# A graph network's prologue: inverse roots by Newton's steps, the first pair of tiles projected ahead of the edge work, edge counts and their gathers moved forward

## The chip, the cores and the metric

The kernel runs on one NeuronCore of a Trainium2 chip, in one launch. The metric is device time in microseconds (us). Engines: PE is TensorE's matmul, PEld its weight load, DVE VectorE, ACT ScalarE, POOL GpSimd, SP SyncE, which here only issues DMAs. ACT and POOL issue DMAs too (ACTq, POOLq and SPq in the profile). Each engine works through its own queue in order; semaphores join the queues.

## The reference

Two layers on x, 3125 nodes of 256 features each: a graph diffusion and a mixture of experts, each on a normalized input and added to what it reads. 103125 directed edges (src, dst), sorted by dst.

```
def _layernorm(x, eps=1e-05):
    m = mean(x, -1);  v = var(x, -1)
    return (x - m) / sqrt(v + eps)

def _spmm(h, src, dst, inv_deg):
    return segment_sum(h[src], dst, 3125) * inv_deg[:, None]

def gnn(h):
    h = silu(h @ W_in.T + b_in)
    out = term = h
    for i in range(1, 7):                       # K_STEPS = 6
        term = _spmm(term, src, dst, inv_deg) / i
        out = out + term
    return out @ W_out.T + b_out

x = x + gnn(_layernorm(x))
x = x + moe(_layernorm(x))                      # 8 experts, the 2 best of each row, 256 -> 512 -> 256
```

The change touches only the beginning: the first layer norm, the projections and the reading of the edges. All else runs the same instructions.

## The kernel before

Nodes stand in 25 tiles of 128 rows (the last has 53). The output projection commutes with the diffusion, so it is applied first: each tile is normalized, multiplied by W_in, put through SiLU, multiplied by W_out, and kept in `t0` as two halves of a number each (a rounded value and what it leaves out, 2 x 256 columns). Then step 1 of the diffusion builds, tile by tile, a dense block of the adjacency matrix out of the edges by products of 0/1 matrices on PE, writes it to memory, and multiplies it with `t0`. Steps 2 to 6 read the blocks back and multiply. In the last step rows are routed to experts, whose matmuls end the kernel.

The prologue, which is all that the change touches, has two strands.

*The projection of tiles.* Tiles of x are loaded into `acc` by SP in groups of 2, 4, 6, 6, 6 and the last one (L321 to L327). DVE takes mean and variance of each (`bn_stats` and `bn_aggr`, L556 and L557, into `mv`). In three batches, tiles 0 to 1, 2 to 5 and 6 to 24, ACT takes the square root of the variance (L558), and DVE its reciprocal `rstd` and the offset `shift` (L559, L560). `normed(t)` (L563 to L573) lets ACT normalize a pair of tiles into `xn` and PE transpose it into `pt`, one pair ahead of its use. The loop over 13 pairs (L576 to L596) copies `pt` to `xt` (ACT, L579), multiplies by `w_in_sb` into `ph` (PE, L586; two halves c, each followed by a SiLU on ACT, L588, into `ht`), multiplies by `w_out_sb` into `pm` (PE, L593), and splits the result into `t0` (DVE, L595 a copy, L596 a subtraction). `ph`, `pm`, `xn`, `xt` and `ht` have one buffer each, `pt` two.

*The edges.* ACT's queue loads `di` (dst) and `si` (src), 128 x 818 numbers each. DVE and ACT cut them into three small parts (L417 to L422), PE transposes these (L433), ACT (parts 0 and 2) and DVE (part 1) copy them side by side into `pairs` (L436, L437), and two DMAs on ACT's queue write the list `edges` of triples to memory (L439, L441). Beside it DVE counts where each group of 16 nodes begins: `first_i` holds the first dst of each chunk of 128 edges; the counts `below` (L447) give a chunk number, POOL gathers that chunk's dst numbers into `row_i` (L455), DVE counts in them (L460, `within`) and has the place `start_i` (L463). With it POOL gathers each group's triples from `edges` into `rec` (L471). Out of `rec` come the place in the window and the lane (`in_w`, `pl_f`, L474, L476), the first place of each node (`max_index`, L485, and minima by doubling, L497 to L502), from which PE makes the degrees (L510) and DVE `inv_deg` (L512, L513; scaled for each step by POOL, L515). PE transposes the places and lanes (L527) and DVE copies them out (L532, L536). `build_tile` (L628) compares them with counters (`right`, L647, and `left`, L638, on DVE), multiplies on PE (L658) and copies the block out on ACT (L662).

The order on each engine's queue is not written by hand. A scheduler places the instructions by its own costs and by the program's order; `tc.issue_after(x)` holds what is issued in it behind instruction x in that placing. Once placed, the queues are fixed: an instruction that waits holds all that stand behind it on its engine.

Of the kernel before, what the change touches and what calls it, by code (L numbers as in the profile page):

```python
# [22 lines left out]
D = 256  # L23
NT = 25
# [3 lines left out]
NCH = (NE + P - 1) // P  # L28
# [8 lines left out]
EPS = 1e-5  # L37
# [3 lines left out]
NG = NT * P // W // 2  # L41
# [225 lines left out]
def tile_gnn_then_moe(  # L267
# [33 lines left out]
    prep = before.enter_context(tc.tile_pool(name="prep", bufs=1))  # L301
# [3 lines left out]
    acc = const.tile([P, NT, D], F32, name="acc")  # L305
    nc.vector.memset(acc[:, NT - 1, :], 0.0)
    first_i = prep.tile([NG, NCH], I32, name="first_i")
    di = prep.tile([P, NCP], I32, name="di")
    nc.scalar.dma_start(di, dst_pm)
    w_in_sb = const.tile([P, 2, D], F32, name="w_in_sb")  # L310
    nc.scalar.dma_start(w_in_sb, w_in.rearrange("(k p) o -> p k o", p=P))
    si = prep.tile([P, NCP], I32, name="si")
    nc.scalar.dma_start(si, src_pm)
    b_in_pm = const.tile([P, 2], F32, name="b_in_pm")
    for c in range(2):
        nc.scalar.dma_start(b_in_pm[:, c:c + 1], b_in[c * P:(c + 1) * P].rearrange("(p a) -> p a", a=1))
    w_out_sb = const.tile([P, 2, D], F32, name="w_out_sb")
# [11 lines left out]
    ident = const.tile([P, P], F32, name="ident")  # L329
    make_identity(nc, ident)  # L330
    eps_sb = const.tile([P, 1], F32, name="eps_sb")
    nc.vector.memset(eps_sb, EPS)
    inv_deg = const.tile([P, STEPS, NT], F32, name="inv_deg")
    big = const.tile([1, 1], I32, name="big")

# [42 lines left out]
    low = keys.tile([NG, 2], F32, name="low")  # L378
# [33 lines left out]
    nc.vector.tensor_copy(ident_h, ident)  # L412


    cb = (NCP + P - 1) // P
    part = prep.tile([P, 3, NCP], F16, name="part")
    nc.vector.tensor_scalar(part[:, 2, :], di, -MID, None, op0=ALU.add)  # L417
# [11 lines left out]
    for v in range(3):  # L429
        pq = ps.tile([P, 1024], F16, name="pk")[:, :cb * P].rearrange("p (c e) -> p c e", e=P)  # L430
        for c in range(cb):
            n = min(P, NCP - c * P)
            nc.tensor.transpose(pq[:n, c, :], part[:, v, c * P:c * P + n], ident_h)  # L433
        n = NCP - (cb - 1) * P
        put = nc.vector.tensor_copy if v == 1 else nc.scalar.copy
        put(pairs[:, :cb - 1, :, v], pq[:, :cb - 1, :])  # L436
        put(pairs[:n, cb - 1, :, v], pq[:n, cb - 1, :])  # L437
    by_chunk = edges.rearrange("(c p) v -> c p v", p=P)
    nc.scalar.dma_start(by_chunk[:(cb - 1) * P].rearrange("(b c) p v -> c b p v", c=P),  # L439
                        pairs[:, :cb - 1])  # L440
    nc.scalar.dma_start(by_chunk[(cb - 1) * P:], pairs[:NCP - (cb - 1) * P, cb - 1])  # L441


    junk = prep.tile([P, NCH], BF16, name="junk")
    below = prep.tile([NG, 2], F32, name="below")
    for g in range(2):
        nc.vector.tensor_scalar(junk[:NG, :], first_i, low[:, g:g + 1], None, op0=ALU.is_lt,  # L447
                                op1=ALU.add, accum_out=below[:, g:g + 1])
    chunk = prep.tile([NG, 2], F32, name="chunk")
    nc.vector.tensor_scalar(chunk, below, -1.0, 0.0, op0=ALU.add, op1=ALU.max)  # L450
    chunk_i = prep.tile([NG, 2], U32, name="chunk_i")
    nc.vector.tensor_copy(chunk_i, chunk)
    row_i = prep.tile([NG, 2, P], I32, name="row_i")
    for g in range(2):
        nc.gpsimd.indirect_dma_start(  # L455
            row_i[:, g, :], None, dst_cm,
            bass.IndirectOffsetOnAxis(ap=chunk_i[:, g:g + 1], axis=0))
    within = prep.tile([NG, 2], F32, name="within")
    for g in range(2):
        nc.vector.tensor_scalar(junk[:NG, :P], row_i[:, g, :], low[:, g:g + 1], None,  # L460
# [85 lines left out]
    intro = ExitStack()  # L546
    proj = intro.enter_context(tc.tile_pool(name="proj", bufs=1, side="right"))
    ps_o = intro.enter_context(tc.tile_pool(name="ps_o", bufs=1, space=bass.MemoryType.PSUM, side="right"))
    ps_t = intro.enter_context(tc.tile_pool(name="ps_t", bufs=2, space=bass.MemoryType.PSUM, side="right"))
    mv = const.tile([P, NT, 2], F32, name="mv")  # L550
    rstd = const.tile([P, NT], F32, name="rstd")
    shift = const.tile([P, NT], F32, name="shift")
    for a, b in ((0, 2), (2, 6), (6, NT)):
        for t in range(a, b):
            st = work.tile([P, 6], F32, name="st")
            nc.vector.bn_stats(st, acc[:, t, :])  # L556
            nc.vector.bn_aggr(mv[:, t, :], st)  # L557
        nc.scalar.activation(rstd[:, a:b], mv[:, a:b, 1], AF.Sqrt, bias=eps_sb, scale=1.0)  # L558
        nc.vector.reciprocal(rstd[:, a:b], rstd[:, a:b])  # L559
        nc.vector.scalar_tensor_tensor(shift[:, a:b], mv[:, a:b, 0], -1.0, rstd[:, a:b],  # L560
                                       op0=ALU.mult, op1=ALU.mult)

    def normed(t):  # L563
        n = min(2, NT - t)
        xn = proj.tile([P, 2, D], F32, name="xn")
        for q in range(n):
            nc.scalar.activation(xn[:, q, :], acc[:, t + q, :], AF.Identity,
                                 bias=shift[:, t + q:t + q + 1], scale=rstd[:, t + q:t + q + 1])
        pt = ps_t.tile([P, 2, 2 * P], F32, name="pt")
        for k in range(2):  # L570
            for q in range(n):
                nc.tensor.transpose(pt[:, k, q * P:(q + 1) * P], xn[:, q, k * P:(k + 1) * P], ident)
        return pt  # L573

    pt = normed(0)
    for t in range(0, NT, 2):  # L576
        n = min(2, NT - t)
        xt = proj.tile([P, 2, 2 * P], F32, name="xt")
        nc.scalar.copy(xt[:, :, :n * P], pt[:, :, :n * P])  # L579
        if t + 2 < NT:  # L580
            pt = normed(t + 2)
        ph = ps_o.tile([P, 2, 2 * P], F32, name="ph")
        ht = proj.tile([P, 2, 2 * P], F32, name="ht")
        for c in range(2):
            for k in range(2):
                nc.tensor.matmul(ph[:, c, :n * P], w_in_sb[:, k, c * P:(c + 1) * P], xt[:, k, :n * P],  # L586
                                 start=(k == 0), stop=(k == 1))
            nc.scalar.activation(ht[:, c, :n * P], ph[:, c, :n * P], AF.Silu,  # L588
                                 bias=b_in_pm[:, c:c + 1], scale=1.0)
        pm = ps_o.tile([P, 2, D], F32, name="pm")  # L590
        for q in range(n):
            for c in range(2):
                nc.tensor.matmul(pm[:, q, :], ht[:, c, q * P:(q + 1) * P], w_out_sb[:, c, :],  # L593
                                 start=(c == 0), stop=(c == 1))
# [507 lines left out]
```

## Time and profile before

| what | value |
|---|---|
| median of three runs | 1346.45 us (1346.13 to 1347.48) |
| the profiled execution's own time | 1345.73 us |
| its span, first to last instruction | 1343.9 us |
| mean granted TensorE clock | 0.966 |
| first multiplication of a block with `t0` (L703) | at 94.83 us |
| step 1 of the diffusion on PE (L703, 625 instructions) | 94.8 to 326.2 us |
| steps 2 to 6 on PE (L1013, 3125 instructions) | 328.4 to 1054.8 us |
| PE busy from 0 to 94.8 us | 71.4 us |
| PE busy from 13.2 to 41.4 us | 20.0 of 28.2 us |
| PE busy from 41.4 to 94.8 us | 51.4 of 53.4 us |

Times of rows are in us from the span's start. A timeline's row gives the start, the busy time, the engine and the line, the operation with its output and inputs, and how often it follows itself; in brackets is the idle time ahead of it and what ended it. A product of fp32 numbers is two records (x4 is two matmuls). Some instructions stand in the queue of an engine (ACTq, SPq, POOLq) without being counted as busy.

Some landings of loads, from the same profile: `first_i` 7.7, `w_in_sb` 8.4, `si` 9.9, tiles 2 to 5 10.8, tiles 6 to 11 14.2, tiles 12 to 17 16.5, tiles 18 to 23 18.9, the last tile 22.2, the edges' two writes 23.7 and 22.2.

### The profile page before, as it was taken

Reading aid. Unit: us, or ns where it says so; the run is one execution under the profiler, and the core shown is the slowest. Engines: PE = TensorE matmul, PEld = TensorE weight load, DVE = VectorE, ACT = ScalarE, POOL = GpSimd, SP = SyncE. Lnnn points to the kernel's source line nnn. Section 1 sums busy time; section 2 is a strip of 40 time slices with the busy share of each in tenths; the row PEclk is TensorE's granted clock in tenths of the full one; section 3 lists DMA queues with packets and bytes.
Section 4 is the critical chain, followed back from the end, with each engine's and each line's share of the span. In section 5 each row is a group of like instructions: output and inputs, shape, how many; then the busy total and the mean of one; then the engine's idle time right before and its main releaser. Section 6 shows DMA issues by size and latency. Waiting matters only on the chain. (4 is left out here: it accounts for less than half of the span.)

```text
span 1343.9 us, 16806 instructions
## 1 busy us (share of the span) xinstructions
PE 1229.9 (92%) x6181; PEld 1015.6 (76%) x6181; DVE 609.5 (45%) x1560; ACT 352.8 (26%) x559; POOL 209.2 (16%) x264
## 2 busy tenths in 40 slices
PE   3999999999999999999999999999999469999940
PEld 2778888887888888888888888887777358888830
DVE  6769999994432222222222222256666512221206
ACT  5756666663000000000000000012222212222210
POOL 2000000008942200000000000002322222222210
PEclk9999999999999999999999999999999769999975
DMA  6023444447888888888888888887887267777737
GB/s 196 1 90 155 171 173 167 176 165 271 347 293 293 295 297 293 294 292 295 294 295 292 296 293 293 294 304 263 283 278 241 76 205 231 226 234 237 223 99 256
DMA packets 86245, 318.47 MB, mean 237 GB/s; under 512 B 12253, under 2 KB 56236, under 8 KB 66952
## 3 DMA queue, kind: packets, MB, share of 16 engines
q1 hardware_dynamic: 74550, 297.14, 62.3%
q0 software_dynamic: 5280, 14.54, 3.0%
q10 hardware_dynamic: 6322, 5.60, 1.3%
q8 instruction: 52, 0.85, 0.2%
q14 instruction: 41, 0.34, 0.1%
HBM read 256.44 MB, written 60.81 MB: 236 GB/s over the span
## 5 line engine op out<-in xcount | busy, mean ns | idle before, releaser
L1013 PE MATMUL pd<-t,blk 128*128 128x512 f32 (+1 forms) x3125 | 710.9, 387 | 3.1 <-DMA blk<-adj 3.1
L1013 PEld LDWEIGHTS pd<-t,blk 128*128 128x128 f32 x3125 | 574.9, 188 | 120.7 <-issue 2.6
L677 DVE SCALAR_TENSOR_TENSOR term<-pd,inv_deg,low 128x256 f32<-128x256 f32 x150 | 72.3, 482 | 437.8 <-ACT low L675 437.7
L675 ACT ACTIVATE low<-pd,inv_deg 128x256 f32<-128x256 f32 x150 | 71.2, 475 | 593.2 <-PE pd L1013 521.1
L703 PE MATMUL pd<-t,blk 128*128 128x512 f32 x625 | 151.1, 398 | 0.0
L662 ACT CAST blk<-pa 128x800 fp32r<-128x800 f32 x98 | 146.7, 1652 | 12.2 <-PE pa L658 12.2
L703 PEld LDWEIGHTS pd<-t,blk 128*128 128x128 f32 x625 | 115.9, 188 | 25.3
L647 DVE TENSOR_TENSOR right<-steps,place 128x800 bf16<-128x800 f16 (+3 forms) x245 | 127.9, 577 | 3.3 <-PE pa L658 3.3
L953 PE MATMUL ph<-xt,w_sb 128*128 128x256 f32 x432 | 100.8, 387 | 2.8 <-DMA w_sb<-in_w_dram 1.7
L658 PE MATMUL pa<-right,left 128*128 128x200 bf16 (+3 forms) x980 | 98.9, 254 | 0.9 <-ACT blk L662 0.9
L962 PE MATMUL py<-w_sb,ht 128*128 128x256 f32 x432 | 97.7, 379 | 0.0
L658 PEld LDWEIGHTS <-left 128*128 128x128 bf16 x980 | 83.4, 97 | 16.4 <-DVE right L647 5.5
L953 PEld LDWEIGHTS ph<-xt,w_sb 128*128 128x128 f32 x432 | 83.7, 195 | 15.1 <-DVE xt L945 3.4
L955 ACT ACTIVATE ht<-ph,b_sb 128x256 f32<-128x256 f32 x108 | 51.1, 474 | 145.0 <-PE ph L953 144.9
L962 PEld LDWEIGHTS py<-w_sb,ht 128*128 128x128 f32 x432 | 80.1, 190 | 9.9
L693 POOL TENSOR_TENSOR early<-t 128x256 f32<-128x256 f32 x50 | 38.0, 771 | 266.6 <-DVE right L647 264.7
L966 POOL DMA_INDIRECT ys<-y,xr x54 | 51.9, 961 | 161.9 <-DVE y L965 141.1
L638 DVE TENSOR_TENSOR left<-steps,lane 128x2560 bf16<-128x2560 f16 x49 | 72.6, 1482 | 1.1 <-PE pa L658 1.1
L945 DVE COPY xt<-px 128x512 f32<-128x512 f32 x27 | 18.7, 692 | 109.9 <-PE px L942 92.1
L847 POOL DMA_INDIRECT xs<-xg,to x50 | 49.0, 980 | 114.0 <-DVE z L789 42.9
L744 POOL IOTA lane_f<- 128x1 f32 x1 | 0.1, 138 | 415.3 <-PE pd L1013 415.3
L352 DVE TENSOR_TENSOR t<-term,t 128x256 fp32r<-128x256 f32 x120 | 55.5, 462 | 0.8
(200 smaller groups left out, 678.1 us busy)
## 6 DMA issues: line engine op xcount, KB each, us to landing
blk<-adj SPq DMA_DIRECT2D x125, 1600.0 KB, 6.7
adj<-blk SPq DMA_DIRECT2D x25, 1536.0 KB, 5.2
w_sb<-in_w_dram SPq DMA_DIRECT2D x54, 512.0 KB, 5.2
xr<-xs SPq DMA_DIRECT2D x27, 257.0 KB, 2.8
got<-ys SPq DMA_DIRECT2D x8, 640.0 KB, 7.2
b_sb<-in_b_dram SPq DMA_DIRECT2D x27, 128.0 KB, 5.0
out_dram<-acc ACTq DMA_DIRECT2D x24, 128.0 KB, 5.0
xs<-pad SPq DMA_DIRECT2D x9, 257.0 KB, 4.2
```

Of the source, the lines that this page charges most:

```text
L352: nc.vector.tensor_sub(dst[:, D:], v, dst[:, :D].bitcast(F32))
L638: nc.vector.tensor_tensor(left.rearrange("p k a l u -> p (k a) l u"), steps[:, None, :P, :].to_broadcast([P, nl, P, 2]), lane[:, h, :, :]. ...
L647: nc.vector.tensor_tensor(r, steps[:, None, :m, :].to_broadcast([P, HALF // 2, m, 2]), place[:, h, k, :].rearrange("p (a u) -> p a u", u=2 ...
L658: nc.tensor.matmul(pa[:, u, lo * NT:hi * NT], left[:, k, a, :, u], right[k][:, a, :, u], start=(k == 0), stop=(k == CK - 1), skip_group_ch ...
L662: nc.scalar.copy(by_dst[:, q:q + 2 * W, :].rearrange("p (u q) i -> p u q i", u=2), pa[:, :, :W * NT].rearrange("p u (q i) -> p u q i", i=NT))
L675: nc.scalar.activation(low, pd[:, D:], AF.Copy, scale=inv)
L677: nc.vector.scalar_tensor_tensor(term, pd[:, :D], inv, low, op0=ALU.mult, op1=ALU.add)
L703: nc.tensor.matmul(pd, blk[:, i * P:(i + 1) * P], t0[:, i, :], start=(i == 0), stop=(i == NT - 1))
L953: nc.tensor.matmul(ph, got[1][:, k, q * P:(q + 1) * P], xt[:, k, :], start=(k == 0), stop=(k == 1))
L962: nc.tensor.matmul(py, ht[:, q, h * P:(h + 1) * P], got[2][:, q, :], start=(q == 0), stop=(q == HT - 1))
L966: nc.gpsimd.indirect_dma_start(ys_at[2 * i + h], bass.IndirectOffsetOnAxis(ap=got[0][:, h, D:].bitcast(U32), axis=0), y, None)
L1013: nc.tensor.matmul(pd[:, :n], blk[:, i * P:(i + 1) * P], old[:, i, :n], start=(i == 0), stop=(i == NT - 2), skip_group_check=True)
```

## The change

- Roots: `norms(a, b)` replaces the square root and the reciprocal by an integer first guess (a shift and a subtraction on the number's bits) and three Newton steps of four operations each. Tiles 0 to 5 do them on DVE; later tiles on POOL, but for the two integer operations and `shift`, which stay on DVE. Batches are now 0 to 1, 2 to 5, 6 to 11, 12 to 17 and 18 to 24, each issued when the pair ahead of it is projected, and held behind the batch before.
- A SiLU on one column at the start takes ACT's table load there.
- `w_in` is loaded ahead of `di`.
- The projection's pools open ahead of the edge work. The counts, the chunk numbers and the gathers of `row_i` come next in the program, then the first pair (`project(0)`), held behind the second count. The edges' parts, transposes, copies and writes are held behind the count and the first pair's matmul and SiLU (`behind`), the copies also behind the second batch of roots.
- The copy of `pm` into `t0` moves from DVE to ACT; the subtraction stays on DVE.

```diff
-    nc.scalar.dma_start(di, dst_pm)
     w_in_sb = const.tile([P, 2, D], F32, name="w_in_sb")
     nc.scalar.dma_start(w_in_sb, w_in.rearrange("(k p) o -> p k o", p=P))
+    nc.scalar.dma_start(di, dst_pm)
...
+    nc.scalar.activation(inv_deg[:, 0, :1], eps_sb, AF.Silu)
...
+    def norms(a, b):
+        on = nc.vector if a < 6 else nc.gpsimd
+        for t in range(a, b):
+            st = work.tile([P, 6], F32, name="st")
+            nc.vector.bn_stats(st, acc[:, t, :])
+            nc.vector.bn_aggr(mv[:, t, :], st)
+        v = proj.tile([P, b - a], F32, name=f"v{a}")
+        on.tensor_scalar(v, mv[:, a:b, 1], EPS, None, op0=ALU.add)
+        half = proj.tile([P, b - a], I32, name=f"half{a}")
+        nc.vector.tensor_scalar(half, v.bitcast(I32), 1, None, op0=ALU.arith_shift_right)
+        r = rstd[:, a:b]
+        nc.vector.tensor_scalar(r.bitcast(I32), half, -1.0, float(0x5f3759df), op0=ALU.mult, op1=ALU.add)
+        q = proj.tile([P, b - a], F32, name=f"q{a}")
+        for _ in range(3):
+            on.tensor_tensor(q, r, r, op=ALU.mult)
+            on.tensor_tensor(q, q, v, op=ALU.mult)
+            on.tensor_scalar(q, q, -0.5, 1.5, op0=ALU.mult, op1=ALU.add)
+            on.tensor_tensor(r, r, q, op=ALU.mult)
+        return nc.vector.scalar_tensor_tensor(shift[:, a:b], mv[:, a:b, 0], -1.0, r,
+                                              op0=ALU.mult, op1=ALU.mult)
...
+    batches = {2: 6, 6: 12, 12: 18, 18: NT}
+    last, seconds = [norms(0, 2)], []
+    turned = [normed(0)]
+
+    def project(t):
+        n = min(2, NT - t)
+        pt = turned.pop()
+        xt = proj.tile([P, 2, 2 * P], F32, name="xt")
+        nc.scalar.copy(xt[:, :, :n * P], pt[:, :, :n * P])
+        if t + 2 in batches:
+            with tc.issue_after(seconds[-1].ins) if seconds else ExitStack():
+                seconds.append(norms(t + 2, batches[t + 2]))
+        if t + 2 < NT:
+            turned.append(normed(t + 2))
...
+        last.extend((p, h))
...
+        nc.scalar.copy(t0[:, t:t + n, :D], pm[:, :n, :])
+        nc.vector.tensor_sub(t0[:, t:t + n, D:], pm[:, :n, :], t0[:, t:t + n, :D].bitcast(F32))
+
+    for g in range(2):
+        last[0] = nc.vector.tensor_scalar(junk[:NG, :], first_i, low[:, g:g + 1], None, op0=ALU.is_lt,
+                                op1=ALU.add, accum_out=below[:, g:g + 1])
...
+        nc.gpsimd.indirect_dma_start(
+            row_i[:, g, :], None, dst_cm,
+            bass.IndirectOffsetOnAxis(ap=chunk_i[:, g:g + 1], axis=0))
+
+    with tc.issue_after(last[0].ins):
+        project(0)
+
+    behind = ExitStack()
+    for one in last[:3]:
+        behind.enter_context(tc.issue_after(one.ins))
...
-        put(pairs[:, :cb - 1, :, v], pq[:, :cb - 1, :])
-        put(pairs[:n, cb - 1, :, v], pq[:n, cb - 1, :])
+        with tc.issue_after(seconds[0].ins):
+            put(pairs[:, :cb - 1, :, v], pq[:, :cb - 1, :])
+            put(pairs[:n, cb - 1, :, v], pq[:n, cb - 1, :])
...
+    behind.close()
...
-    for a, b in ((0, 2), (2, 6), (6, NT)):
...
-        nc.scalar.activation(rstd[:, a:b], mv[:, a:b, 1], AF.Sqrt, bias=eps_sb, scale=1.0)
-        nc.vector.reciprocal(rstd[:, a:b], rstd[:, a:b])
...
-        nc.vector.tensor_copy(t0[:, t:t + n, :D], pm[:, :n, :])
-        nc.vector.tensor_sub(t0[:, t:t + n, D:], pm[:, :n, :], t0[:, t:t + n, :D].bitcast(F32))
+    for t in range(2, NT, 2):
+        project(t)
```

More of the change, by code (lines that the diff above doesn't have):

```diff
@@ L412, in tile_gnn_then_moe @@
     nc.vector.tensor_copy(ident_h, ident)
+    intro = ExitStack()
+    proj = intro.enter_context(tc.tile_pool(name="proj", bufs=1, side="right"))
+    ps_o = intro.enter_context(tc.tile_pool(name="ps_o", bufs=1, space=bass.MemoryType.PSUM, side="right"))
+    ps_t = intro.enter_context(tc.tile_pool(name="ps_t", bufs=2, space=bass.MemoryType.PSUM, side="right"))
+    mv = const.tile([P, NT, 2], F32, name="mv")
+    rstd = const.tile([P, NT], F32, name="rstd")
+    shift = const.tile([P, NT], F32, name="shift")
@@ new lines, in normed @@
+    def normed(t):
+        n = min(2, NT - t)
+        xn = proj.tile([P, 2, D], F32, name="xn")
+        for q in range(n):
+            nc.scalar.activation(xn[:, q, :], acc[:, t + q, :], AF.Identity,
+                                 bias=shift[:, t + q:t + q + 1], scale=rstd[:, t + q:t + q + 1])
+        pt = ps_t.tile([P, 2, 2 * P], F32, name="pt")
+        for k in range(2):
+            for q in range(n):
+                nc.tensor.transpose(pt[:, k, q * P:(q + 1) * P], xn[:, q, k * P:(k + 1) * P], ident)
+        return pt
@@ new lines, in tile_gnn_then_moe @@
+    batches = {2: 6, 6: 12, 12: 18, 18: NT}
+    last, seconds = [norms(0, 2)], []
+    turned = [normed(0)]
+    def project(t):
+        n = min(2, NT - t)
+        pt = turned.pop()
[6 more added lines that the diff above has]
+            turned.append(normed(t + 2))
+        ph = ps_o.tile([P, 2, 2 * P], F32, name="ph")
+        ht = proj.tile([P, 2, 2 * P], F32, name="ht")
+        for c in range(2):
+            for k in range(2):
+                p = nc.tensor.matmul(ph[:, c, :n * P], w_in_sb[:, k, c * P:(c + 1) * P], xt[:, k, :n * P],
+                                     start=(k == 0), stop=(k == 1))
+            h = nc.scalar.activation(ht[:, c, :n * P], ph[:, c, :n * P], AF.Silu,
+                                     bias=b_in_pm[:, c:c + 1], scale=1.0)
+        last.extend((p, h))
+        pm = ps_o.tile([P, 2, D], F32, name="pm")
+        for q in range(n):
+            for c in range(2):
+                nc.tensor.matmul(pm[:, q, :], ht[:, c, q * P:(q + 1) * P], w_out_sb[:, c, :],
+                                 start=(c == 0), stop=(c == 1))
+        nc.scalar.copy(t0[:, t:t + n, :D], pm[:, :n, :])
+        nc.vector.tensor_sub(t0[:, t:t + n, D:], pm[:, :n, :], t0[:, t:t + n, :D].bitcast(F32))
@@ new lines, in tile_gnn_then_moe @@
+    junk = prep.tile([P, NCH], BF16, name="junk")
+    below = prep.tile([NG, 2], F32, name="below")
+    for g in range(2):
+        last[0] = nc.vector.tensor_scalar(junk[:NG, :], first_i, low[:, g:g + 1], None, op0=ALU.is_lt,
+                                op1=ALU.add, accum_out=below[:, g:g + 1])
+    chunk = prep.tile([NG, 2], F32, name="chunk")
+    nc.vector.tensor_scalar(chunk, below, -1.0, 0.0, op0=ALU.add, op1=ALU.max)
+    chunk_i = prep.tile([NG, 2], U32, name="chunk_i")
+    nc.vector.tensor_copy(chunk_i, chunk)
@@ L415, in tile_gnn_then_moe @@
+    row_i = prep.tile([NG, 2, P], I32, name="row_i")
+    for g in range(2):
+        nc.gpsimd.indirect_dma_start(
[6 more added lines that the diff above has]
+        behind.enter_context(tc.issue_after(one.ins))
     cb = (NCP + P - 1) // P
@@ L441, in tile_gnn_then_moe @@
     nc.scalar.dma_start(by_chunk[(cb - 1) * P:], pairs[:NCP - (cb - 1) * P, cb - 1])
[L444 to L457, printed above, removed]
+    behind.close()
     within = prep.tile([NG, 2], F32, name="within")
@@ L542, in tile_gnn_then_moe @@
                                             reuse_waits="tile"))
[L546 to L552, printed above, removed]
@@ L553, in tile_gnn_then_moe @@
-    for a, b in ((0, 2), (2, 6), (6, NT)):
[L554 to L558, printed above, removed]
-        nc.vector.reciprocal(rstd[:, a:b], rstd[:, a:b])
-        nc.vector.scalar_tensor_tensor(shift[:, a:b], mv[:, a:b, 0], -1.0, rstd[:, a:b],
-                                       op0=ALU.mult, op1=ALU.mult)
@@ L563, in normed @@
[L563 to L594, printed above, removed]
-        nc.vector.tensor_copy(t0[:, t:t + n, :D], pm[:, :n, :])
-        nc.vector.tensor_sub(t0[:, t:t + n, D:], pm[:, :n, :], t0[:, t:t + n, :D].bitcast(F32))
+    for t in range(2, NT, 2):
+        project(t)
```

## The prediction

> **What bounds the kernel now.** I read the busy times first, then a table of stretches, then the timelines of PE, ACT, DVE and POOL up to 95 us.
>
> ```profile
> span 1343.9 us, 16806 instructions
> PE 1229.9 (92%) x6181; PEld 1015.6 (76%) x6181; DVE 609.5 (45%) x1560; ACT 352.8 (26%) x559; POOL 209.2 (16%) x264
> ```
> PE sets the time. Every instruction behind the first few tiles of diffusion stands in the same order before and after, so the change is worth what it does to PE's idle time ahead of them.
>
> ```profile
> 10.00:20.00 10.00, 4.29 (x25) 2.79 (x25) 10.00 (x47) 6.41 (x10) 1.49 (x2) 1.00 0.85 270
> 20.00:30.00 10.00, 7.34 (x28) 5.60 (x28) 6.48 (x32) 6.38 (x10) 2.75 (x3) 1.00 0.38 115
> 30.00:40.00 10.00, 6.97 (x22) 4.81 (x22) 9.54 (x29) 7.81 (x16) 0.00 (x0) 0.66 0.07 25
> 40.00:50.00 10.00, 9.61 (x63) 7.63 (x64) 9.44 (x24) 8.74 (x26) 1.73 (x5) 1.00 0.01 2
> 50.00:60.00 10.00, 9.88 (x56) 7.95 (x55) 6.57 (x16) 6.35 (x11) 0.00 (x0) 1.00 0.00 1
> ```
> After the stretch, the columns are its length, then PE, PEld, DVE, ACT and POOL busy, the granted clock, the DMA share and GB/s. From 40 us PE is full; all that can be won lies before that.
>
> ```profile
> 20.37 2.08 PE L586 MATMUL ph<-xt,w_in_sb 128*128 128x256 f32 x4 [2.50 <-ACT xt L579]
> ...
> 26.68 1.03 PE L586 MATMUL ph<-xt,w_in_sb 128*128 128x256 f32 x4
> 32.37 2.08 PE L586 MATMUL ph<-xt,w_in_sb 128*128 128x256 f32 x4 [4.66 <-ACT ht L588]
> ...
> 41.37 0.20 PE L510 MATMUL pk<-in_tile,deg_at 100*128 100x25 f16 x2
> ```
> The same four records take 1.03 us, and 2.08 behind a pause of 4.66 us (clock 0.66 in that stretch). The pause comes from ACT, which sat behind one square root:
>
> ```profile
> 18.54 0.39 ACTq L439 DMA_DIRECT2D edges<-pairs  x1
> ...
> 30.22 0.31 ACT L558 ACTIVATE rstd<-mv,eps_sb 128x19 f32<-128x19 f32 x1 [3.43 <-DVE mv L557]
> 30.55 1.28 ACT L588 ACT_TABLE_LOAD   x1
> ```
> The edge records go to memory at 18.54, are gathered on POOL at 25.88, and end as degrees that PE needs at 41.37 (L510). DVE and POOL on that path:
>
> ```profile
> 23.96 0.35 DVE L460 TENSOR_SCALAR_CACHE_REDUCE junk<-row_i,low 100x128 bf16<-100x128 int32 x1 [3.49 <-DMA row_i<-in_dst_cm_dram,chunk_i]
> ...
> 30.68 0.55 DVE L474 TENSOR_SCALAR in_w<-rec,low_h 100x648 f16<-100x648 f16 x1
> ...
> 39.65 0.19 DVE L500 TENSOR_TENSOR least<-least 100x26 f32<-100x26 f32 x1
> ...
> 39.95 0.18 DVE L500 TENSOR_TENSOR least<-least 100x18 f32<-100x18 f32 x1
> ```
> ```profile
> 4.77 0.33 POOL L480 COPY listed<-digits 100x16 f32<-100x16 f32 x2
> 18.20 1.22 POOL L455 DMA_INDIRECT row_i<-in_dst_cm_dram,chunk_i  x1 [13.11 <-DVE mv L557]
> ...
> 25.88 1.00 POOL L471 DMA_INDIRECT rec<-edges,start_i  x1 [5.14 <-DVE start_i L463]
> ...
> 42.23 1.97 POOL L515 TENSOR_SCALAR inv_deg<-inv_deg 128x25 f32<-128x25 f32 x5 [14.04 <-DVE inv_deg L513]
> ```
>
> **The change, part by part.** The order on each engine is from the built program, the durations from the rows above.
>
> *Roots.* Three square roots (0.3 us each) and three of the four table loads (1.28 each) leave ACT. A batch now needs 16 small operations, each on the result of the one before. On DVE such a chain steps by 0.2 us (39.65 to 39.95 holds one dependent step of 0.2 and a free one of 0.1). On POOL no row is as small as 128x6. Copies of 100x16 take 0.188 us (mean of the two), operations on 128x25 0.354, with some 0.08 between starts and ends. The step is thus between 0.20 (DVE's) and 0.43; I take 0.188+0.08 = 0.27, the copy being nearer in size.
> The Trainium skill (GPSIMD Engine Reference, section 4.1) advises VectorE over GPSIMD for elementwise work, about twice as fast with two inputs. Here the addition on 128x256 takes 0.771 us on POOL against 0.462 on DVE; with DVE's step everywhere the sum below would fall by about 2 us.
>
> *First pair.* Tiles 0 and 1 land at 6.08. Statistics 0.9, 16 steps of 0.2: shift at 10.1 (12.8 now). Two normalizations 1.1, four transposes about 1.1, the copy 0.6: first projection at 12.9 (20.37 now), at 2.08 per half on a cold PE. It leaves PE at about 19.6, not at 26.6. The new w_in load ahead of di costs nothing: both are in before DVE's part at 14.5 (w_in took 7.2 us to land, di is read at 6.75 now).
>
> *Gathers forward, edges back.* Both counts (1.04 each) stand right behind the first shift: chunk numbers at 13.7, first gather at 13.8 instead of 18.20. It lands 5.7 us later as now (18.20 to 23.96), at 19.5. DVE's reduction of it stands ahead of the second batch's roots, so DVE waits from 16.6; behind it are start numbers at 20.1, 12 steps (2.4) and the first pair's subtraction (0.6): second shift at 22.9. ACT must normalize the second pair (1.0) before it copies the last part of the edges (1.5): the edges' DMA issues at 25.5 instead of 18.54. About 5.1 us of landing (the median of such issues): 30.6. ACT's two issues (1.0) stand ahead of pair 1's copy.
>
> *POOL.* Its queue has the third batch's roots ahead of the records' gather. DVE ends their statistics at 27.1 (pairs copy 1.5, six tiles at 0.43), then 13 POOL steps and two hops to DVE (0.5): 31.1. So the gather starts at 31.1, 5.2 later than 25.88; at 4.6 us more the first records are in at 35.7 (30.5 now).
>
> *To the degrees.* Now 30.5 to 41.2, 10.7 us. Out of that stretch go the copies of two pairs (0.69 each), a subtraction and the reciprocal work, some 2.5; in come six tiles' statistics (2.6), two more subtractions (1.3) and a wait for the fourth batch's roots (0.7): net 2.1. Degrees on PE at 35.7+12.8 = 48.5, against 41.4: 7.1 later. But PE is further by then: pairs 0 to 4 are multiplied but for pair 4's second product; now it is pairs 0 to 2 but for three quarters of pair 2's second product. A pair without tile building costs 4.1 us (4.75 from 59.24 to 63.99, less 0.65 of building), so PE is 2x4.1-0.4 = 7.8 ahead. Net here: -0.7.
>
> *The last batch.* The shift of tiles 18 to 24 stands on DVE ahead of the first tile's operands and pair 4's subtraction. POOL does five scalings of degrees first (1.97, from 49.7), then 12 steps (3.2): 54.9. Right and left (1.9) and the subtraction (0.7) follow; pair 5's second product needs that buffer: 57.6. PE is there at 54.9 and stands 2.7, after another 0.9 for ACT's activation: 3.6. The like pauses now are about 0.5. Net 3.1.
>
> *Rest.* Copies of the products move from DVE (0.69 each) to ACT (about 0.6): covered by ACT's idle half per pair, except at the last tile, where they stand between the copies of blocks: 0.9 more idle before diffusion starts.
>
> Sum: -0.7+3.1+0.9 = +3.3. On the profiled execution's own 1345.73 (span 1343.9 and 1.8 around it) that is 1349.0; the median of the runs is 0.7 above it, so 1349.7.
>
> **Rivals.** *No change.* A POOL step of 0.20 takes 0.5 off the records (the edges' landing at 30.6 then binds) and 0.8 off the last shift; the faster of today's gathers (19.73 to 24.29, 4.6) takes up to 0.9 more: +1.1, so 1347.5. For it: DVE and the smallest POOL rows step that fast. Against: the 128x25 row.
>
> *Faster.* The two pairs that PE is ahead could be kept. That takes the records by about 33 instead of 35.7, and the last shift not waited for: -0.7-2.7+0.9 = -2.5, and 1 to 2 more if PE stays warm, for 1342.5. It decides at the records' gather, from 28.4 on. For it: 8.2 us of PE idle between 13.2 and 41.4, of which the 4.66 in front of L588 surely goes. Against: every DVE wait in the order above.
>
> *Slower still.* At a POOL step of 0.42 the gather comes 2.0 later and the last shift 1.8, and PE's pause grows to 4.5, like the 4.66 that cost 2.3 us by doubled matmuls: 3.3+3.8+2.3 = +9.4, so 1355.8. The Trainium skill (TensorE: Matmul & The Clock Gate, "What's actually happening") has the clock halved after an idle window of about 3.4 us; by that the pause need not grow so far.
>
> *The gathers come earlier and bring nothing* is part of my forecast: the records wait for the edges, not for the counts.
>
> **How the numbers follow.** Forecast (+1.5 to +6) 0.47, no change 0.25, faster 0.13, slower still 0.15. 0.2% is 2.7 us, about what can be told from no change. Faster by more 0.13; of the forecast's share about 0.07 lies below 2.7, so within 0.32 and slower 0.55. The range goes from 1345.0 (past no change, toward the faster case) to 1356.0 (the dear POOL step).
>
> **What would show it.** Right: the records' gather near 31 and behind the third batch's roots; edges issued near 25.5; PE at the degrees near 48.5; DVE idle some 4 us at the last shift with POOL as releaser; diffusion's fifth tile 2 to 5 us later. Wrong: gather before 28.5, POOL steps under 0.2 us, or no PE pause after the degrees.

## The result, and the profile after

| | before | after |
|---|---|---|
| median of 13 runs each | 1345.51 us (1344.07 to 1358.92) | 1355.64 us (1350.14 to 1368.01) |
| after over before, 95% interval | | 1.0089 (1.0063 to 1.0115) |
| the profiled execution | 1345.73 us | 1353.86 us |
| its mean granted clock | 0.966 | 0.962 |
| degrees on PE | 41.37 us | 51.86 us |
| first product of a block with `t0` | 94.83 us | 100.27 us |
| first product of the fifth tile | 133.33 us | 142.01 us |
| steps 2 to 6 on PE | 726.4 us | 726.8 us |

The change makes the kernel slower by about 10 us; 1349.7 was forecast. In the profiled pair 8.1 us are lost, and 8.7 us of lateness are there when step 1's fifth tile begins; behind it the lateness stays between 8.1 and 10.2 us to the end. Of the 13 runs, nine lie at 1350.1 to 1356.3 and four at 1365.6 to 1368.0; these four are taken up at the end. Of the runs shown further below, one of e_act_changed (1383 us) and one of e_act_shift (1375 us) lie more than 1.5% above the fastest of their kernel, count as slow and are left out of ratios and ranges.

The busy times and the stretches of the kernel after (columns as before: length, then PE, PEld, DVE, ACT and POOL busy, granted clock, DMA share, GB/s):

```profile
span 1352.1 us, 16863 instructions
PE 1236.1 (91%) x6181; PEld 1018.8 (75%) x6181; DVE 606.6 (45%) x1582; ACT 355.0 (26%) x567; POOL 216.6 (16%) x303
```
```profile
10.00:20.00 10.00, 8.54 (x30) 5.74 (x31) 5.66 (x33) 4.20 (x9) 2.41 (x2) 1.00 0.81 263
20.00:30.00 10.00, 4.62 (x26) 3.29 (x24) 7.12 (x32) 6.24 (x11) 1.69 (x9) 0.75 0.21 68
30.00:40.00 10.00, 8.43 (x35) 5.99 (x34) 6.58 (x22) 6.91 (x16) 4.29 (x13) 0.90 0.27 78
40.00:50.00 10.00, 7.51 (x29) 5.88 (x28) 7.20 (x34) 5.24 (x11) 1.57 (x7) 0.83 0.01 2
50.00:60.00 10.00, 7.00 (x52) 5.43 (x50) 5.91 (x19) 9.12 (x28) 3.99 (x18) 0.96 0.01 2
60.00:70.00 10.00, 9.62 (x35) 7.41 (x36) 7.43 (x16) 3.07 (x6) 0.00 (x0) 0.70 0.00 0
```

The same number of products keeps PE busy for 6 us longer. Before 20 us PE has more to do than before (8.54 us of 10 against 4.29); from 40 to 60 us it is busy for 14.5 us where it was for 19.5. The clock, which fell once before (0.66 from 30 to 40 us), is down in five of the six stretches. Busy time in the last row is high because the clock is low: 9.62 us for 35 records.

PE's timeline after, around its pauses (start, busy time, in brackets the idle time ahead and what ended it):

```profile
27.44 2.07 PE L479 MATMUL ph<-xt,w_in_sb 128*128 128x256 f32 x4 [2.59 <-ACT xt L469]
...
45.92 3.48 PE L487 MATMUL pm<-w_out_sb,ht 128*128 128x256 f32 x8 [1.69 <-DVE t L490]
...
51.86 0.20 PE L598 MATMUL pk<-in_tile,deg_at 100*128 100x25 f16 x2
...
52.79 1.96 PE L487 MATMUL pm<-w_out_sb,ht 128*128 128x256 f32 x8
...
60.38 1.22 PE L487 MATMUL pm<-w_out_sb,ht 128*128 128x256 f32 x2 [2.69 <-DVE t L490]
...
62.15 2.77 PE L487 MATMUL pm<-w_out_sb,ht 128*128 128x256 f32 x6
64.71 1.69 PE L479 MATMUL ph<-xt,w_in_sb 128*128 128x256 f32 x4
```

The same eight records of `pm` take 1.96 us at 52.79 and 3.48 us behind the pause of 1.69. Both later pauses are ended by DVE's subtraction (L490), which frees the one buffer of `pm`. Why that was late stands on DVE's and POOL's timelines:

```profile
18.70 0.35 DVE L548 TENSOR_SCALAR_CACHE_REDUCE junk<-row_i,low 100x128 bf16<-100x128 int32 x1 [3.81 <-DMA row_i<-in_dst_cm_dram,chunk_i]
...
31.33 0.17 DVE L446 SCALAR_TENSOR_TENSOR shift<-mv,rstd 128x6 f32<-128x6 f32 x1 [3.40 <-POOL rstd L445]
...
42.11 0.17 DVE L446 SCALAR_TENSOR_TENSOR shift<-mv,rstd 128x6 f32<-128x6 f32 x1 [1.49 <-POOL rstd L445]
...
57.67 0.17 DVE L446 SCALAR_TENSOR_TENSOR shift<-mv,rstd 128x7 f32<-128x7 f32 x1 [3.59 <-POOL rstd L445]
57.75 0.57 DVE L684 TENSOR_TENSOR right<-steps,place 128x800 bf16<-128x800 f16 x1
58.24 1.48 DVE L675 TENSOR_TENSOR left<-steps,lane 128x2560 bf16<-128x2560 f16 x1
59.64 0.68 DVE L490 TENSOR_TENSOR t<-pm,t 128x512 fp32r<-128x512 f32 x1
```
```profile
31.10 0.20 POOL L445 TENSOR_TENSOR rstd<-rstd,q 128x6 f32<-128x6 f32 x1
31.90 1.08 POOL L559 DMA_INDIRECT rec<-edges,start_i  x1 [0.61 <-issue]
...
57.14 0.21 POOL L444 TENSOR_SCALAR q<-q 128x7 f32<-128x7 f32 x1
57.43 0.20 POOL L445 TENSOR_TENSOR rstd<-rstd,q 128x7 f32<-128x7 f32 x1
```

DVE's queue waits for POOL at these three offsets (`shift`), 8.5 us in all, and once for the gather moved forward, 3.8 us. At 54.08 it reaches the last batch's offset and stands there until 57.67; the first tile's operands and the subtraction that PE needs stand behind that instruction, and the subtraction ends at 60.3, when PE goes on.

### The profile page after: what moved, and what is told of

It reads as the page before. It is cut to its first block, busy times and chain, and to the rows that moved or that the text cites. A ratio compares the mean times of both kernels' runs of the same rounds, so it can differ in the third digit from the quotient of the medians.

```text
span 1352.1 us, 16863 instructions
## 1 busy us (share of the span) xinstructions
PE 1236.1 (91%) x6181; PEld 1018.8 (75%) x6181; DVE 606.6 (45%) x1582; ACT 355.0 (26%) x567; POOL 216.6 (16%) x303
## 5 line engine op out<-in xcount | busy, mean ns | idle before, releaser
L699 ACT CAST blk<-pa 128x800 fp32r<-128x800 f32 x98 | 146.8, 1653 | 13.9 <-PE pa L695 13.8
L990 PEld LDWEIGHTS ph<-xt,w_sb 128*128 128x128 f32 x432 | 83.5, 194 | 14.2 <-DVE xt L982 2.6
L724 DVE TENSOR_TENSOR acc<-acc,term 128x256 f32<-128x256 f32 x125 | 55.7, 446 | 0.2
```

Of the source, the lines that this page charges most:

```text
L699: nc.scalar.copy(by_dst[:, q:q + 2 * W, :].rearrange("p (u q) i -> p u q i", u=2), pa[:, :, :W * NT].rearrange("p u (q i) -> p u q i", i=NT))
L724: nc.vector.tensor_add(acc[:, j, :], acc[:, j, :], term)
L990: nc.tensor.matmul(ph, got[1][:, k, q * P:(q + 1) * P], xt[:, k, :], start=(k == 0), stop=(k == 1))
```

## The experiments

They ran on four chips, some of which take longer in the last steps of the diffusion (up to 742 us for steps 2 to 6, in e_free_edges, where the trace before has 726), so times are given as ratios to the kernel before on the same chip, and the traces are compared at the first product of step 1's fifth tile. Between executions that mark moves too: it is 142.0, 142.5 and 141.0 in three profiles with the changed prologue, 133.3 and 135.1 in two of the prologue before. "Idle" and "busy" are PE's from its first instruction to that mark.

| kernel | degrees on PE | fifth tile | idle | busy | time over before (95%) |
|---|---|---|---|---|---|
| before | 41.4 | 133.3 | 10.1 | 110.0 | 1 |
| changed | 51.9 | 142.0 | 16.5 | 115.3 | 1.0089 (1.0063 to 1.0115) |
| e_changed: changed, again | 53.3 | 142.5 | 16.6 | 115.5 | 1.0079 (1.0053 to 1.0105) |
| e_dve_roots: all roots on DVE | 46.5 | 131.1 | 9.1 | 111.4 | 0.9991 (0.9959 to 1.0023) |
| e_last_dve: last batch's on DVE | 52.5 | 136.4 | 13.2 | 112.7 | 1.0023 (1.0004 to 1.0042) |
| e_shift: last shift moved back | 50.6 | 137.1 | 14.2 | 112.6 | 1.0123 (1.0108 to 1.0138) |
| e_t0_dve: copy of `pm` on DVE | 49.5 | 135.6 | 13.3 | 112.2 | 0.9997 (0.9976 to 1.0018) |
| e_pm2: two buffers of `pm` | 48.3 | 132.6 | 11.0 | 111.2 | 0.9981 (0.9963 to 0.9998) |
| e_pt1: one of `pt`, one of `pm` | 48.6 | 133.3 | 12.1 | 110.8 | 1.0009 (0.9976 to 1.0041) |
| e_fill: PE's pause filled | 50.5 | 139.0 | 13.9 | 114.6 | 1.0112 (1.0077 to 1.0148) |
| e_free_edges: edges not held back | 47.2 | 143.2 | 19.0 | 112.2 | 1.0082 (1.0050 to 1.0115) |
| e_counts_back: gathers not forward | 54.5 | 138.1 | 11.2 | 112.6 | 1.0050 (1.0016 to 1.0084) |
| e_sqrt: square roots again | 50.4 | 142.2 | 18.0 | 111.4 | 1.0148 (1.0105 to 1.0190) |

Between before and changed PE's idle time grows by 6.4 us and its busy time by 5.3, and PE starts 3.0 us earlier (10.2 instead of 13.2); together that is the 8.7 us.

The theory: Newton's chains on POOL hold DVE's queue at `shift`; what stands behind it there reaches PE late; PE pauses, and after the pause works at half clock.

**POOL or DVE.** All roots on DVE:

```diff
-        on = nc.vector if a < 6 else nc.gpsimd
+        on = nc.vector
```

> The changed kernel with every batch of roots on DVE, none on POOL. Theory (DVE waits for chains of small POOL operations, and PE for DVE; three waits of 3.4, 1.5 and 3.6 us at shift in the changed kernel's trace): a DVE step is 0.2 us where POOL's is 0.28 with hops on top, and POOL's gather of the records no longer stands behind a chain. So the records' gather starts by 30 (31.9 now), PE is at the degrees near 48 (51.9), no DVE wait at the last shift, the fifth tile of diffusion 5 to 8 us earlier, near 135 (142.0): 0.998 to 1.003 of the kernel before. Rival (the copy of the products on ACT holds the buffer): the pauses of PE ahead of the second product stay, fifth tile at 140 or later, ratio 1.006 or more. Rival (the edges are simply late): degrees on PE no earlier than 50, ratio 1.005 or more.

The fifth tile comes at 131.1, 10.9 us earlier than in the changed kernel and 2.2 earlier than before. DVE does as many steps more as POOL does fewer, and yet the three later offsets wait 0.04 us at most: where DVE has other work, it does that between two dependent steps. Its timeline in this run:

```profile
57.07 0.16 DVE L444 TENSOR_SCALAR q<-q 128x7 f32<-128x7 f32 x1
57.14 0.57 DVE L684 TENSOR_TENSOR right<-steps,place 128x800 bf16<-128x800 f16 x1
57.62 0.16 DVE L445 TENSOR_TENSOR rstd<-rstd,q 128x7 f32<-128x7 f32 x1
57.70 0.67 DVE L684 TENSOR_TENSOR right<-steps,place 128x1000 bf16<-128x1000 f16 x1
```

The step on `q` ends, an operand of a tile is built, the next step follows 0.55 us later. Here each step takes 0.08 us of DVE's time ahead of the next instruction; with the chains on POOL, DVE waited 1.5 to 3.6 us for each. But in this run the scheduler also put the fourth and the last batch's `shift` behind a subtraction that frees `pm`, so engine and order both changed; e_pt1 below tells them apart.

Then the last batch alone (`on = nc.gpsimd if a in (6, 12) else nc.vector`):

> The changed kernel with only the last batch's roots (tiles 18 to 24) on DVE; the third and fourth batch stay on POOL. The prediction's account (3.1 us of the loss from the last batch's wait): DVE's wait of 3.59 us ahead of the last shift goes, the fifth tile at 136 to 139 us instead of 142.0, time 1.000 to 1.005. Rival (the third batch's chain, with the records' gather behind it, is the dear one): the fifth tile at 140 to 142, time 1.006 to 1.010.

136.4: of the 10.9 us that all roots on DVE bring, this batch brings 5.6. The degrees stay at 52.5; the other 5.3 us come only when the third and fourth batch, ahead of the degrees, go to DVE too. The scheduler, given another batch, also moved some of step 1's operands, so the next run moves as little as can be.

**One instruction.** The last batch stays on POOL; only its `shift` is held behind the fifth pair's subtraction:

```diff
+    subs = {}
...
-        return nc.vector.scalar_tensor_tensor(shift[:, a:b], mv[:, a:b, 0], -1.0, r,
-                                              op0=ALU.mult, op1=ALU.mult)
+        with tc.issue_after(subs[{18: 8}[a]].ins) if a in {18: 8} else ExitStack():
+            return nc.vector.scalar_tensor_tensor(shift[:, a:b], mv[:, a:b, 0], -1.0, r,
+                                                  op0=ALU.mult, op1=ALU.mult)
...
-        nc.vector.tensor_sub(t0[:, t:t + n, D:], pm[:, :n, :], t0[:, t:t + n, :D].bitcast(F32))
+        subs[t] = nc.vector.tensor_sub(t0[:, t:t + n, D:], pm[:, :n, :], t0[:, t:t + n, :D].bitcast(F32))
```

> The changed kernel with the last batch's shift held behind the fifth pair's subtraction; nothing else is altered, and POOL's chain takes as long. Theory (that one instruction, waiting for POOL ahead of the first tile's operands and the subtraction, makes PE's pause of 2.69 us and the halved clock behind it): DVE does right, left and the subtraction while POOL works, the pause at 60 us and the clock's fall go, the fifth tile at 135.5 to 138 us instead of 142.0, time 1.000 to 1.004. Rival (PE would stand for the last tiles' shift anyway, or for the late records): 140 to 142, time 1.006 to 1.010.

DVE's and PE's timelines of that run:

```profile
53.23 1.49 DVE L678 TENSOR_TENSOR left<-steps,lane 128x2560 bf16<-128x2560 f16 x1
54.64 0.68 DVE L493 TENSOR_TENSOR t<-pm,t 128x512 fp32r<-128x512 f32 x1
57.95 0.17 DVE L449 SCALAR_TENSOR_TENSOR shift<-mv,rstd 128x7 f32<-128x7 f32 x1 [2.63 <-POOL rstd L447]
```
```profile
56.28 0.59 PE L490 MATMUL pm<-w_out_sb,ht 128*128 128x256 f32 x2
58.76 0.48 PE L698 MATMUL pa<-right,left 128*128 128x250 bf16 x3 [1.88 <-DVE right L687]
59.08 1.46 PE L490 MATMUL pm<-w_out_sb,ht 128*128 128x256 f32 x6
```

DVE still waits 2.63 us for POOL, but has subtracted at 55.3, so `pm` starts at 56.28 instead of 60.38 and its six records take 1.46 us, not 2.77. The fifth tile comes at 137.1, 4.9 us earlier. Of these, 1.2 us lie ahead of the degrees, where the clock did not fall in this execution; the place of one instruction is worth some 4 us, and the pair e_act_changed and e_act_shift below says the same (141.0 and 137.2). The measured time, 1.0123, lies far outside what was expected. The profiled run has a stall of 12 us in step 2, shown at the end, and the other three lie within 1 us of it; whether they had the stall too was not profiled. With the stalled instruction moved (e_act_shift, below) the time is 1.0019, within what was expected here.

**The coupling through `pm`.** Two buffers of `pm`, paid for by one of `pt`:

```diff
-        pm = ps_o.tile([P, 2, D], F32, name="pm")
+        pm = ps_o.tile([P, 2, D], F32, name=f"pm{t // 2 % 2}")
...
-    ps_t = intro.enter_context(tc.tile_pool(name="ps_t", bufs=2, space=bass.MemoryType.PSUM, side="right"))
+    ps_t = intro.enter_context(tc.tile_pool(name="ps_t", bufs=1, space=bass.MemoryType.PSUM, side="right"))
```

> The changed kernel with two buffers for pm (and one for pt to pay for it); POOL's chains, the late records and every operation stay. Theory (DVE, held by POOL's roots, is late with the subtraction that frees pm, so PE pauses ahead of the second product and then runs it at half clock): the pauses of 1.69 and 2.69 us at pm end, and the two falls of the clock behind them; the fifth tile's first product at 133 to 137 us instead of 142.0, time 0.997 to 1.003 of the kernel before. Rival (the records come late and that is what costs): the degrees stay behind 48 us, the fifth tile at 140 to 142, time 1.006 to 1.010.

132.6, though the records' gather (31.96) and the degrees (48.3) remain late: the late records are not what costs. That looks like the second buffer, but with one buffer of `pt` the scheduler also places things differently: the fourth batch's and the last batch's `shift` now stand behind a subtraction. The control has the change of `pt` alone:

> The changed kernel with one buffer for pt and one for pm: the control for the run with two buffers of pm, since the scheduler places the last shift behind the subtraction and the operands there too. If the second buffer of pm brought that gain: pauses ahead of pm's products and the fifth tile at 137 to 142 us. If it was DVE's order: the fifth tile at 131 to 134 as with two buffers (132.6), time 0.997 to 1.001.

133.3 with one buffer of `pm`. DVE's timeline of that run:

```profile
43.74 0.68 DVE L490 TENSOR_TENSOR t<-pm,t 128x512 fp32r<-128x512 f32 x1
...
44.83 0.17 DVE L446 SCALAR_TENSOR_TENSOR shift<-mv,rstd 128x6 f32<-128x6 f32 x1 [0.28 <-POOL rstd L445]
...
53.66 0.69 DVE L490 TENSOR_TENSOR t<-pm,t 128x512 fp32r<-128x512 f32 x1
...
58.81 0.17 DVE L446 SCALAR_TENSOR_TENSOR shift<-mv,rstd 128x7 f32<-128x7 f32 x1 [2.67 <-POOL rstd L445]
```

Both subtractions stand ahead of the `shift` that waits for POOL, and PE has no pause of over 1 us at `pm` behind 40 us. So DVE's order brings nearly all of it, and the second buffer 0.7 us at most, less than two executions differ by. The reading of e_pm2 as a test of the buffer falls; the theory of DVE's queue is the stronger for it. And since every chain of the later batches is still on POOL here, order brings 8.7 of the 10.9 us of e_dve_roots, and the engine at most the 2.2 us that are left.

**The copy of `pm`.** Back to DVE (`nc.vector.tensor_copy` for `nc.scalar.copy`), all else as changed:

> The changed kernel with the copy of the products into t0 back on DVE. Theory (POOL chains): the last shift still holds DVE by 3 to 4 us and the buffer is still freed behind it, so at most 2 us come back from the copy's own latency: fifth tile at 139 to 142, ratio 1.005 to 1.009. Rival (the copy on ACT): the first buffer waits disappear, PE's pauses ahead of the second product shrink from 1.7 and 2.7 us to under 1 each, and the clock is not lowered at 44 to 50: fifth tile near 136, ratio 1.000 to 1.004.

135.6, the rival's number: the theory had expected 139 or more. The placing explains it in part, since here too the last `shift` moved behind the subtraction (DVE waits 1.36 us at it, not 3.59). How much is the copy itself is not settled.

**The clock.** Repeats of transposes that PE has done already fill its last pause; nothing comes earlier by them (the hand-over of `xn` in `normed` is left out here):

```diff
...
+        for _ in range({10: 6}.get(t, 0)):
+            ptn, xnn = turned[-1]
+            for k in range(2):
+                for q in range(min(2, NT - t - 2)):
+                    nc.tensor.transpose(ptn[:, k, q * P:(q + 1) * P], xnn[:, q, k * P:(k + 1) * P], ident)
         pm = ps_o.tile([P, 2, D], F32, name="pm")
```

> The changed kernel, with the four transposes of the seventh pair repeated on PE ahead of the sixth pair's second product, so that PE works through most of the pause of 2.69 us that ended at 60.38; nothing comes earlier by it. Theory (half the loss is the halved clock behind the pauses): the granted clock in 60 to 68 us is 0.9 or more instead of 0.50 and 0.74, two records of pm take 1.0 us and not 1.8, the fifth tile at 139 to 140.5 us instead of 142.0. Rival (the clock costs nothing, since PE would wait for DVE's next subtraction anyway): the fifth tile at 141.5 to 142.5.

PE's timeline of that run:

```profile
46.03 1.99 PE L492 MATMUL pm<-w_out_sb,ht 128*128 128x256 f32 x8 [1.69 <-DVE t L495]
...
56.15 1.91 PE L488 MATMUL pt<-ident,xn 128*128 128x128 f32 x16
58.99 1.99 PE L492 MATMUL pm<-w_out_sb,ht 128*128 128x256 f32 x8 [0.94 <-DVE t L495]
```

The clock stays at 1.00 from 40 us on and the fifth tile comes at 139.0, 3.0 us earlier, with more work on PE. Of these 1.4 us were not brought by the filling: behind the pause at 46, as long as in the changed kernel, the clock did not fall in this execution, and the degrees came at 50.5. Behind the degrees the way to the fifth tile is 88.5 us instead of 90.2; as the scheduler also put the first tile's products behind `pm` there, these 1.7 us are not certainly the clock's alone. Its measured time, 1.0112, is above the changed kernel's all the same. Its eight runs fall into two clusters: 1361 to 1362, some 7.5 us above the kernel before (1354.3) where the trace shows 5.7 at the fifth tile, and 1372 to 1377, higher by 11 to 15 us, near the size of the stall shown at the end. Only a run of the lower cluster was profiled.

**The other parts of the change.** The edges' copies and writes not held back (`issue_after` left out there):

> The changed kernel without the orders that hold the edges' parts, transposes and copies behind the first pair and the second batch of roots; the scheduler places them by itself. Rival (edges are simply late): edges written 4 to 6 us earlier, records' gather near 26, PE at the degrees 4 us earlier and the fifth tile with it, ratio 1.003 or less. Theory (POOL chains in DVE's order): records earlier, but the chains still stand ahead of DVE's work and PE is less far with its pairs when the degrees come: fifth tile within 2 us of 142, ratio 1.005 to 1.011.

The records' gather starts at 25.3, the degrees come at 47.2, and the fifth tile at 143.2, no better: PE pauses 4.47 and 5.64 us for `xn`, and ACT, which makes `xn`, stands still 5.43 and 4.37 us for the second and the third batch's `shift`. The third batch's first guess now stands on DVE behind the records' work, so POOL's chain for it starts at 41.8 instead of 28.0. Earlier records alone do not cure it; whether holding the edges back gains anything is not shown. Then the counts and gathers back behind the edges' writes, with the first pair still ahead:

> The changed kernel with the edge counts and their gathers back behind the edges' writes, as they were. Theory: the gathers moved forward bring nothing, since the records wait for the edges and for POOL; moved back, DVE's wait for row_i at 14.6 to 18.7 goes away and the edges are written 3 us earlier, but the second gather then follows the first by a full round trip, so the records come at 35 to 38 instead of 31.9; PE is further with its pairs at the degrees: fifth tile within 2 us of 142, ratio 1.006 to 1.012. Rival (the early gather is what makes the prologue shorter): 4 us later or more, ratio 1.012 or more.

The records are used 6.5 us later than in the changed kernel, at 43.3, and the fifth tile comes 4 us earlier. One cost of the gathers moved forward is seen at the second pair: DVE stands for `row_i` ahead of the second batch's roots, and the pair's transposes start at 23.82 instead of 19.98. But the scheduler also put the last `shift` ahead of the degrees in this run, where DVE waits 1.15 us for it and not 3.59; how much of the 4 us is the gathers' place stays open. Last, the square root on ACT and the reciprocal in place of Newton's steps, in the new batches:

> The changed kernel with the square root on ACT and the reciprocal on DVE in place of Newton's steps, in the same five batches; all else as changed. Theory: each of the batches then costs ACT a square root and two table loads (0.3 + 2 x 1.28 = 2.9 us), about 4 x 2.9 us between the first pair and the sixth, on an ACT that is 60 to 95% busy there, so PE pauses behind it: the fifth tile at 137 to 142 us, time 1.003 to 1.010; the steps off ScalarE are a gain by themselves, and only where they stand on POOL do they cost. Rival (Newton's steps as such cost more than the square roots): the fifth tile at 132 to 136, time 0.998 to 1.002.

142.2, no better than changed, by another way (its four runs, too, lie in two clusters, at 1355 to 1357 and 1371 to 1374, whence the 1.0148). ACT's and PE's timelines:

```profile
40.18 1.28 ACT L435 ACT_TABLE_LOAD   x1
41.48 0.30 ACT L435 ACTIVATE rstd<-mv,eps_sb 128x7 f32<-128x7 f32 x1
...
43.68 1.28 ACT L472 ACT_TABLE_LOAD   x1
```
```profile
45.50 2.07 PE L470 MATMUL ph<-xt,w_in_sb 128*128 128x256 f32 x4 [4.67 <-ACT ht L472]
```

A root takes two table loads with it, and PE pauses 4.67 us behind the last. With the same five batches on DVE (e_dve_roots) the mark was 11.1 us earlier. So taking the roots off ACT is a gain; the loss is in where they went and who waits for them.

**The changed kernel again, and with step 2's cast on ACT.**

> The changed kernel once more, on the chip of the runs beside it. If the profile of the result was typical: the fifth tile's first product at 141 to 143 us, the granted clock down in 44 to 48 and in 60 to 68 us, time 1.006 to 1.011 of the kernel before. If the clock's fall behind a pause of 1.7 us is chance, as one run with the same pause and a full clock behind it suggests: no fall in 44 to 48 us, and the fifth tile 1 to 2 us earlier.

142.5 and 1.0079: the result was typical. Its clock fell behind the 1.68 us pause again, as in the typical case; that the fall is chance all the same is seen from the four other profiles with this pause, told at the end. Its profile shows the stall of step 2, so four more kernels had the first cast of a finished tile moved to ACT in steps 2 to 6:

```diff
...
-            split(new[:, j, :], term)
+            split(new[:, j, :], term, nc.vector.tensor_copy if step == 1 else nc.scalar.copy)
```

> The kernel before with that cast on ACT in steps 2 to 6: the control. Theory: its prologue is as it was and the stalled cast was rare there (2 of 30 runs), so 0.998 to 1.001. If ACT's cast costs or brings something by itself in steps 2 to 6, it shows here.

> The changed kernel with the first cast of a finished tile (L353) on ACT in steps 2 to 6; the order of the prologue and of step 1 is as changed. Theory (two things make the loss: 8.7 us before the fifth tile in every run, and in some runs 12 us where that cast stands 24 us on DVE beside POOL's additions): no run lies 10 us above the others, the fifth tile at 142, time 1.005 to 1.0075 of the kernel before. Rival (the jump of 12 us has another cause than the cast): jumps remain in a third of the runs, time 1.008 to 1.011.

> The kernel with the last shift held behind the fifth pair's subtraction, whose four runs all had the stalled cast (1.0123), with that cast on ACT in steps 2 to 6. Theory: its fifth tile stays near 137.1, no run jumps, and the time is 1.002 to 1.004 of the kernel before (3.7 us of 1347); against the changed kernel with the same cast on ACT 4 to 6 us less. Rival (the shift's place brings nothing to the end, or the jump isn't the cast): 1.006 or more.

> The changed kernel with all roots on DVE and that cast on ACT in steps 2 to 6. Theory: the fifth tile at 131 us, 2.2 before the kernel before, and no run jumps: 0.997 to 0.9995. Rival (what the prologue gains is given back by step 2): 1.000 to 1.003.

| with the cast on ACT | fifth tile | time over the kernel before (95%) |
|---|---|---|
| before | 135.1 | 0.9998 (0.9978 to 1.0017) |
| changed | 141.0 | 1.0084 (1.0054 to 1.0114) |
| last shift moved back | 137.2 | 1.0019 (0.9991 to 1.0046) |
| all roots on DVE | 131.5 | 1.0006 (0.9975 to 1.0038) |

The cast's place costs nothing by itself, and the one moved `shift` now reaches the end: 0.65% of 1355, some 9 us, between the intervals' middles, and the two intervals do not meet; the traces show 4 us. What was expected of the jumps failed: with the cast on ACT two runs of the changed kernel still lie at 1374 and 1378 where the others lie at 1359 to 1370, and two with all roots on DVE at 1366 and 1370 where the others lie at 1351 to 1357. So the stalled cast is not the cause of all jumps. That the roots on DVE beat the kernel before is not shown: 2 us at the fifth tile, and intervals that hold 1. Only e_pm2's interval (0.9963 to 0.9998) lies below 1, and barely, as one of sixteen such intervals; all roots on DVE with two buffers of `pm` were no better:

> The changed kernel with all roots on DVE and two buffers for pm (one for pt). Theory: no wait of DVE for POOL is left and DVE's lateness reaches PE one pair later, so the fifth tile comes at 128 to 131 us (all roots on DVE alone gave 131.1, the kernel before 133.3): time 0.996 to 0.999. Rival (with POOL out of the way pm's single buffer costs nothing more): 131 to 132, time 0.998 to 1.001.

131.1 at the fifth tile, 0.9998 (0.9971 to 1.0025).

## Why the prediction was right or wrong

The direction and the mechanism of the waits were right, the size was not, and the clock behind the pauses was left out: +3.3 us forecast at the fifth tile, +8.7 measured.

- *First pair.* First `shift` 7.97 (10.1 forecast), because tiles 0 and 1 landed at 4.0, not at 6.08; first projection 12.20 (12.9), ACT's new table load at 8.09 to 9.37 having taken back most of that.
- *Gathers and edges.* First gather 12.18 (13.8), DVE's wait for `row_i` 3.81 from 14.9 on to 18.70 (16.6 to 19.5), start numbers 19.98 (20.1), second shift 22.92 (22.9), edges issued 25.62 (25.5). Right.
- *POOL.* Step 0.28 us (0.27), the records' gather behind the third batch's roots at 31.90 (31.1). Right. An operation on 128x6 numbers took 0.20 us there, on DVE 0.16 to 0.17 on 128x4: near each other, unlike the operations on 128x256 that the prediction compares (where its 0.462 us is DVE's subtraction; DVE's addition took 0.445).
- *To the degrees: the step that failed first.* 51.86 instead of 48.5. The records were in use at 36.83 (35.7); DVE's wait for the fourth batch was 1.49 (0.7); and a subtraction waited 1.38 us for ACT's copy of a product that ran at half clock. PE had as many pairs done as forecast, so this part cost 10.5 - 7.8 = +2.7 us where -0.7 was put.
- *The last batch.* DVE's wait 3.59 (about 4), PE's pause 2.69 (2.7). The pause was right and its price was not: it was put down as idle time alone, and the clock's fall only into a rival, for pauses from 4.5 us on. From the degrees to the fifth tile the forecast comes to 91.96 - 7.8 + 3.1 + 0.9 = 88.2 us; with the clock kept up (e_fill) the way took 88.5, in the changed kernel 90.2.
- So of the 5.4 us that were missed, about 3.0 are the clock behind pauses of 1.7 and 2.7 us (e_fill, one profile each, where the mark moves by 1.5 us between executions), 1.1 the records and 0.8 the fourth batch's wait. The clock's part ahead of the degrees shows in seven profiles: where it stayed up behind the pause at 46 us, the degrees came at 50.5 to 50.7, where it fell, at 51.9 to 53.3.
- *Rivals.* "Faster" fell at its own condition, the records' gather before 28.4. "Slower still" came near the time (1355.8) with the wrong condition: POOL's step wasn't dearer. That the measured 1355.6 lies within the range, which goes to 1356.0 for that dear step, is luck. "The gathers come earlier and bring nothing" may have been too mild (e_counts_back, where the last `shift` moved too).

The way that PE's pauses took was seen: POOL's chain, DVE's queue, the subtraction, the buffer of `pm`. The forecast also names the last `shift`'s place on DVE; what it does not say, and the runs show, is that this place alone is worth some 4 us, and the order of two `shift`s nearly all of the loss (e_pt1).

## What to carry to other kernels

A chain of small dependent operations that is sent to an idle engine is dear if its result is taken by a busy engine whose queue goes on behind it. Look first where the instruction stands that takes the result: with the chains left on POOL, its place brought back 8.7 of 10.9 us here, and the chains on DVE, between other work, 2.2 at most. And price a pause of PE with what follows it: beside pauses of 1.7 and 2.7 us the lower clock cost about 3 us more.

## What the runs showed of the hardware

*The clock falls behind short pauses, by chance.* Seven profiles have the same pause of 1.68 to 1.70 us ahead of `pm` at 46 us. In three the next eight records took 3.48 to 3.78 us, in four 1.99. Behind the pauses of 2.64 to 2.71 us at 59 to 62 us the clock fell in three profiles of three; behind the 1.88 and 1.90 us in the two with the moved `shift`, and the 2.11 and 2.00 us at 34 and 38 us in e_sqrt, it did not. The Trainium skill (TensorE: Matmul & The Clock Gate, "What's actually happening") has the clock judged over a window of 3.4 us that runs freely, which fits the chance; that a whole idle window is needed does not fit a fall behind 1.7 us of idle time.

*A cast on DVE stood for 24 us beside POOL.* DVE's timelines of e_changed, and a stretch of the same run:

```profile
347.24 24.48 DVE L353 CAST t<-term 128x256 fp32r<-128x256 f32 x1
371.64 0.41 DVE L724 TENSOR_TENSOR acc<-acc,term 128x256 f32<-128x256 f32 x1
```
```profile
364.00:368.00 4.00, 0.00 (x0) 0.00 (x0) 4.00 (x1) 0.00 (x0) 4.00 (x7) 0.80 0.94 368
```

The cast takes 0.29 us as a rule (median of 120). Here it lasts until the unbroken row of POOL's additions on `early` ends: the cast ends 0.15 us after the row's first gap, of 0.08 us, begins. PE stands meanwhile: step 2's first five tiles take 41.95 us instead of 29.58. The profile of e_shift has the like (23.59 us, 41.57, and the same 0.15 us); in the twelve others with this cast on DVE it takes 0.93 us at most. The Trainium skill (SBUF — State Buffer, "Who interferes with whom") has the two engines share a port pair, held for an instruction. That fits, if the cast lost the pair to some 35 additions in a row (24.48 us at 0.70 each); no run shows the ports themselves. Four of the 13 runs of the result lie 12 us above the rest, one of 13 before lies 13 above; the size fits this stall, but none of them was profiled, and with the cast on ACT some jumps remained.
